# A graph-attention kernel with the logit columns of its weight matrices made by TensorE instead of VectorE, and a new order of its head and tail

## The chip, the cores and the metric

The kernel runs on one core of one Trainium2 chip. The metric is the device time of one execution in microseconds; the kernel before took 2969.14 us (median of three runs, 2966.99 to 2972.52).

## The reference, cut to what matters

```python
# x: 64 x 256 x 512, adj: 64 x 256 x 256 (about 3% ones)
h = relu(layernorm(x))
x = x + gat(gat_elu(h, W1, att_src1, att_dst1, b1), W2, att_src2, att_dst2, b2)   # mask: adj or diagonal
h = relu(layernorm(x))
x = x + relu_att(h, W_proj, W_att, b_att)                                         # mask: adj

def gat(...):                       # per graph; 4 heads of 256 for W1, one head of 512 for W2
    xl = h @ W
    asrc, adst = (xl * a_src).sum(-1), (xl * a_dst).sum(-1)      # one logit per node and head
    e = leaky_relu(asrc[:, None] + adst[None, :], 0.2), masked
    out = softmax(e, axis=source).T @ xl + bias
# relu_att is the same with 8 heads of 64, a vector of 2 x 64 per head in W_att, a bias b_att on the logit
```

A logit is a product of `h` with a column `W[:, head] @ a[head]`. Such columns depend on the weights alone: 4 + 4 of them for `W1`, 1 + 1 for `W2`, 8 + 8 for `W_proj`.

## The kernel before, in words

Each of the 64 graphs has 256 nodes, two tiles of 128 rows. A graph goes through three projections, `m1a` and `m1b` (512 to 1024, two halves), `m2` (1024 to 512) and `m3` (512 to 512). Each is a Strassen-Winograd product of 2 x 2 blocks: seven products `p1` to `p7` on TensorE (PE) of two (`m1`, `m3`) or four (`m2`) fp32 matmuls each, with left operands combined by GpSimd (`left`), right operands (`right`, four subtractions of a weight tile) made once by VectorE, and the partial sums evicted by ScalarE (`q1`, `q6`, `q7`, `q4`) and VectorE (`q2`, `c22`, `q3`). The weights lie in SBUF as `w1_sb` (a, b), `w2_sb` and `wp_sb`, seven blocks each, four of them loaded and three made. The logit columns stand in front of the weights of a block, so that the products yield the logits too.

After a projection a layer goes: exponentials of the logits (`exp`), their rows written to DRAM (`ship`) and read back to all partitions (`rows`), attention weights (`edges`: a scaled copy by ScalarE into one of two PSUM buffers `wys`, then a maximum and mask by VectorE), the matmul with the values (`gat`), and division and bias (`out`). Between layers the features are turned: for most graphs through DRAM (`away`/`home`, `send2`/`take2`) and a VectorE transpose (`back`), for the first and last graph in part by TensorE transposes (`turn`).

The order on every engine's queue is written out by hand. `run` goes through a text of steps such as `0 m1b p2` (graph offset, step, arguments) and issues them; every engine works its own instructions strictly in that order. `head` runs once, `order` for each of 61 rounds, `tail` once. Steps of `w` belong to the class `Weights` (L627 of before). PSUM has four rotating buffers `pm` and two `sum`.

Ahead of `head` stand the loads: graph 0 and the weights on the queues of SP and ACT, the attention vectors each copied to all 128 partitions (L604, L607, L616), and the norm of graph 0. In `head` before, `dots1` (L636) and `dots2` make each logit column by VectorE: `dot` (L595) multiplies a 128 x 256 block of weights with a vector copied to all partitions and sums it, 32 times for `W1` and 32 for `W2`; `columns2` adds halves; `dots3` (L665) multiplies on GpSimd and reduces on VectorE, 16 times. The products of graph 0 that use raw blocks only are issued between them.

## Time and profile before

| what | value |
|---|---|
| median of three runs | 2969.14 us |
| the profiled execution: own time, span | 2968.22 us, 2966.4 us |
| granted TensorE clock, mean of the span | 0.996 |
| PE busy in 0 to 20, 20 to 40, 40 to 60 us | 5.76, 13.54, 12.94 us |
| VectorE busy in 0 to 20, 20 to 40, 40 to 60, 60 to 80 us | 10.30, 17.91, 19.72, 19.48 us |
| ScalarE busy in the same stretches | 3.89, 2.61, 10.43, 6.93 us |
| PE busy in 2900 to 2920, 2920 to 2940, 2940 to 2950, 2950 to 2966.4 us | 20.00, 14.83, 7.96, 6.77 us |
| first PE instruction, last PE instruction start | 11.30 us, 2959.71 us |
| memory traffic in the first 30 us | 200 to 410 GB/s after 3 us |

The span runs from the first to the last instruction of one profiled execution; about 1.8 us of that execution's own time lie outside it. A line of the chain gives start, duration and what ran; PE is TensorE's matmul, DVE VectorE, ACT ScalarE, POOL GpSimd, SP the engine that issues most DMAs. An fp32 matmul shows as two records. "Idle before" names how long an engine stood still ahead of an instruction, and what released it.

### The profile page before, as it was taken

To read this page: it belongs to the slowest core of one execution; us is meant where nothing else is said; L and a number is where in the kernel's file an instruction comes from. 1 tells how busy PE (TensorE), PEld (TensorE's weight loads), DVE (VectorE), ACT (ScalarE), POOL (GpSimd) and SP (SyncE) were. 2 spreads that over 40 slices of the span, in tenths; PEclk is the share of its full clock that TensorE was granted. 3 is DMA by queue.
4 is the path that set the end of the run, shared out by engine and by line. 5 is a ranking of instruction groups with operands and counts; after the bars stand their busy time and mean duration, and the time that the engine had idled before them with its cause. 6 is when DMAs were issued, how large, how long until landed. Compare 5 with 4: busy or idle time off the path is not lost.

```text
span 2966.4 us, 59522 instructions
## 1 busy us (share of the span) xinstructions
PE 2917.8 (98%) x20296; PEld 2531.6 (85%) x20296; DVE 2531.3 (85%) x6370; ACT 1711.3 (58%) x4489; POOL 1287.4 (43%) x1882
## 2 busy tenths in 40 slices
PE   6999999999999999999999999999999999999997
PEld 4888888888888888888888888888888888888886
DVE  8788888888888888888888888888888888888886
ACT  3466565655655655655656556556556556555554
POOL 3443443444444444434444444444444344344433
PEclk9999999999999999999999999999999999999998
DMA  6556555656565665555556565565555556566542
GB/s 193 155 173 180 175 180 171 180 178 179 170 182 176 175 180 174 172 180 177 179 171 185 173 179 173 178 184 167 175 177 174 178 178 179 172 182 176 179 136 73
DMA packets 536859, 513.17 MB, mean 173 GB/s; under 512 B 85736, under 2 KB 373352, under 8 KB 536552
## 3 DMA queue, kind: packets, MB, share of 16 engines
q1 hardware_dynamic: 535176, 507.20, 57.5%
q8 instruction: 165, 2.70, 0.4%
q10 hardware_dynamic: 1376, 2.10, 0.2%
q14 instruction: 142, 1.16, 0.1%
HBM read 332.01 MB, written 168.79 MB: 169 GB/s over the span
## 4 chain that ended last, share of the span: by engine, by line
PE 97%; DVE 1%; DMA 1%; issue 0%; ACT 0%; POOL 0%; SPq 0%; ACTq 0%; DVEq 0%
PE sum L55 38%; PE pm L55 29%; PE pm L411 15%; PE pm L556 8%; PE pm L481 7%; DVE prod L597 0%; DMA w1a_sb<-in_L_gnn_W_dram 0%; DMA xs<-in_x_dram 0%; DMA h<-kept_h 0%; DMA z<-kept_z 0%; DVE e L292 0%; DVE hs L213 0%; ACT h L199 0%; DVE z L419 0%; DMA bc<-kept 0%
## 5 line engine op out<-in xcount | busy, mean ns | idle before, releaser
L291 ACT ACTIVATE wys<-bc,exs_sb 128x256 f32<-128x256 f32 x1646 | 715.4, 468 | 297.4 <-DMA bc<-kept 145.4
L61 ACT ACTIVATE kept<-sum 128x260 f32<-128x260 f32 (+3 forms) x768 | 296.0, 386 | 714.0 <-PE sum L55 713.3
L292 DVE SCALAR_TENSOR_TENSOR e<-wys,exs_sb,cap 128x256 f32<-128x256 f32 x1024 | 444.9, 476 | 62.2 <-ACT wys L291 52.6
L55 PE MATMUL sum<-w_sb,h1s 128*128 128x257 f32 x2048 | 488.1, 380 | 0.6
L411 PE MATMUL pm<-xl,e 128*128 128x257 f32 x2048 | 476.4, 380 | 0.9 <-DVE e L292 0.8
L411 PEld LDWEIGHTS pm<-xl,e 128*128 128x128 f32 x2048 | 387.9, 190 | 60.1 <-DVE e L292 1.7
L55 PEld LDWEIGHTS sum<-w_sb,h1s 128*128 128x128 f32 x2048 | 383.3, 190 | 64.3 <-issue 3.8
L566 POOL TENSOR_TENSOR x<-x,o 128x256 f32<-128x256 f32 x256 | 182.0, 731 | 486.5 <-DVE o L564 484.6
L261 DVE TENSOR_TENSOR xl<-pm,kept 128x256 f32<-128x256 f32 (+2 forms) x768 | 318.1, 415 | 79.1 <-ACT kept L61 40.4
L219 POOL TENSOR_TENSOR hs<-hs 128x256 f32<-128x256 f32 x128 | 109.0, 852 | 617.9 <-DVE hs L213 589.8
L55 PE MATMUL pm<-w_sb,h1s 128*128 128x257 f32 x1536 | 361.6, 384 | 0.0
L55 PEld LDWEIGHTS pm<-w_sb,h1s 128*128 128x128 f32 x1536 | 285.8, 189 | 44.8 <-POOL h1s L219 1.0
L213 DVE STREAM_TRANSPOSE hs<-h 128x512 f32<-128x512 f32 x252 | 283.2, 1150 | 8.4 <-DMA h<-kept_h 8.0
L292 DVE SCALAR_TENSOR_TENSOR e<-wys,exs_sb,mask 128x256 f32<-128x256 f32 x640 | 278.4, 477 | 12.9 <-ACT wys L291 7.0
L449 DVE STREAM_TRANSPOSE h1s<-z 128x512 f32<-128x512 f32 x252 | 260.6, 1104 | 17.6 <-DMA z<-kept_z 17.6
L55 PE MATMUL sum<-w1a_sb,hs 128*128 128x260 f32 x1024 | 269.1, 386 | 4.0 <-DVE w1a_sb L597 3.4
L55 PE MATMUL sum<-wp_sb,hs 128*128 128x264 f32 x1024 | 271.0, 387 | 0.7 <-ACT hs L229 0.7
L55 PE MATMUL sum<-w1b_sb,hs 128*128 128x256 f32 x1024 | 266.4, 383 | 4.9 <-DVE r L417 2.6
L556 PEld LDWEIGHTS pm<-xl,e 128*64 128x64 f32 x8192 | 245.9, 138 | 24.8 <-issue 24.1
L419 DVE SCALAR_TENSOR_TENSOR z<-pm,r,b_sb 128x256 f32<-128x256 f32 x512 | 247.7, 484 | 18.3 <-DVE r L417 0.3
L219 POOL TENSOR_TENSOR h1s<-h1s 128x512 f32<-128x512 f32 x64 | 81.3, 1270 | 412.2 <-DVE h1s L449 405.2
L556 PE MATMUL pm<-xl,e 128*64 128x65 f32 x8192 | 255.8, 223 | 1.9 <-DVE e L292 1.7
(94 smaller groups left out, 4832.0 us busy)
## 6 DMA issues: line engine op xcount, KB each, us to landing
bc<-kept SPq DMA_DIRECT2D x380, 256.0 KB, 4.6
kept_h<-h SPq DMA_DIRECT2D x126, 512.0 KB, 3.5
h<-kept_h SPq DMA_DIRECT2D x126, 512.0 KB, 3.7
kept_z<-z SPq DMA_DIRECT2D x252, 256.0 KB
z<-kept_z SPq DMA_DIRECT2D x252, 256.0 KB, 2.9
xs<-in_x_dram SPq DMA_DIRECT2D x64, 512.0 KB, 6.0
x<-in_x_dram SPq DMA_DIRECT2D x64, 512.0 KB
out_dram<-x SPq DMA_DIRECT2D x64, 512.0 KB
```

The lines of the kernel that those rows point to most:

```text
L55: self.nc.tensor.matmul(to[:, :self.n], self.lhs[:, i, c, :], self.rhs[:, i, c, :], start=(first and c == 0), stop=(last and c == self.nk ...
L61: self.nc.scalar.activation(s[:, :self.n], self.sum[:, :self.n], AF.Copy)
L213: nc.vector.transpose(a[:, 4 * t:4 * t + 2].rearrange("p r k (j q) -> p q (r k) j", q=4), h[:, t].rearrange("p (q i c) -> p q c i", q=4, c=4))
L219: nc.gpsimd.tensor_tensor(s1, s3, a22, ALU.add)
L261: nc.vector.tensor_tensor(dst, pm, add, ALU.add)
L291: nc.scalar.activation(wy, bc, AF.Copy, scale=yw)
L292: nc.vector.scalar_tensor_tensor(dst, wy, xw, mask, ALU.max, op)
L411: nc.tensor.matmul(pm[:, :Q + 1], self.e[1, h][:, s, t * P:(t + 1) * P], xl1[:, s, h, L1:], start=(s == 0), stop=(s == T - 1))
L419: nc.vector.scalar_tensor_tensor(self.zt[t][:, sl], pm[:, :Q], r, b1_sb[:, sl], ALU.mult, ALU.add)
L449: nc.vector.transpose(a.rearrange("p k (j q) -> p q k j", q=4), z.rearrange("p (q i c) -> p q c i", q=4, c=4))
L481: nc.tensor.matmul(pm[:, :n], self.e[2][:, s, t * P:(t + 1) * P], xl2[:, s, half, L2:L2 + n], start=(s == 0), stop=(s == T - 1))
L556: nc.tensor.matmul(pv[q:q + 64, h, :], self.e[3, a * G + h][:, s, t * P + q:t * P + q + 64], xl3[:, s, a * G + h, :], start=(s == 0), stop ...
```

## The change

The attention vectors are no longer copied to all partitions. Six small DMAs on ACT's queue bring them as 32 rows of 128 elements (`vec_sb`). One TensorE transpose turns them, and 26 small ScalarE copies lay them out as stationary operands `va` for the three layers (`lay`), with zeros around a head's entries for layers 1 and 3 (two more memsets on GpSimd).

A block of weights (512 x 128 elements) is turned by four transposes and copied from PSUM by ScalarE (`turnw`, 20 in all: 8 for `W1`, 8 for `W2`, 4 for `W_proj`). `dotw` multiplies it with its part of `va`: one matmul with 8, 2 or 16 stationary and 512 moving columns, accumulating over the blocks of a layer. `cols` copies the sum from PSUM, turns it back with four small transposes and copies the columns into the weight tiles (2 or 4 ScalarE copies). `dot`, `dots1`, `dots2`, `columns2`, `load3` and `dots3` are gone. The subtractions `sums1`, `sums2` and `sums3` remain.

`head` and `tail` are written out anew; `order`, which runs 61 times, is unchanged. In the new head the steps of graph 0's `m1` come after the dots of layers 1 and 2; turning and dots of `W_proj` stand later, among graph 0 and graph 1. In the new tail the same steps stand in another order.

```diff
+    vec_sb = const.tile([32, P], F32, name="vec_sb")
+    va = [const.tile([P, 8, 2, H1], F32, name="va1"), const.tile([P, 4, 2], F32, name="va2"),
+          const.tile([P, 4, 2, 2, G], F32, name="va3")]
+    nc.gpsimd.memset(va[0], 0.0)
+    nc.gpsimd.memset(va[2], 0.0)
...
-    def dot(dst, u, v):
-        prod = work.tile([P, Q], F32, name="prod", bufs=2)
-        nc.vector.tensor_tensor_reduce(prod, u, v, 1.0, 0.0, ALU.mult, ALU.add, dst)
...
+    nc.scalar.dma_start(vec_sb[0:8, :], att_src1.rearrange("h (i f) -> (h i) f", f=P))
+    nc.scalar.dma_start(vec_sb[8:16, :], att_dst1.rearrange("h (i f) -> (h i) f", f=P))
+    nc.scalar.dma_start(vec_sb[16:20, :], att_src2.rearrange("o (i f) -> (o i) f", f=P))
+    nc.scalar.dma_start(vec_sb[20:24, :], att_dst2.rearrange("o (i f) -> (o i) f", f=P))
+    for j in range(2):
+        nc.scalar.dma_start(vec_sb[24 + 4 * j:28 + 4 * j, :].rearrange("i (l k) -> i l k", l=2),
+                            w_att.rearrange("(i l) (j k) -> i j l k", l=2, j=2)[:, j])
 
     graphs[0].load()
-    nc.scalar.dma_start(att1[0].rearrange("p h f -> p (h f)"), rows_of(att_src1, HF))
     for r in range(2):
         bring(w1_sb[1], w1, 2 * Q, r, (nc.sync, nc.scalar))
-    nc.scalar.dma_start(att1[1].rearrange("p h f -> p (h f)"), rows_of(att_dst1, HF))
...
-    for a, src in zip(att2, (att_src2, att_dst2)):
-        nc.sync.dma_start(a, rows_of(src, D2))
...
+        def lay(self):
+            pm = ps_mm.tile([P, 512], F32, name="pm")
+            nc.tensor.transpose(pm[:, :32], vec_sb, ident[:32, :32])
+            for j in range(2):
+                for h in range(H1):
+                    nc.scalar.activation(va[0][:, 2 * h:2 * h + 2, j, h], pm[:, 8 * j + 2 * h:8 * j + 2 * h + 2], AF.Copy)
+                nc.scalar.activation(va[1][:, :, j], pm[:, 16 + 4 * j:20 + 4 * j], AF.Copy)
+                for i in range(4):
+                    for l in range(2):
+                        q = slice(64 * l, 64 * l + 64)
+                        nc.scalar.activation(va[2][q, i, i // 2, 1 - j, 2 * (i % 2) + l:2 * (i % 2) + l + 1],
+                                             pm[q, 24 + 4 * j + i:25 + 4 * j + i], AF.Copy)
...
+        def turnw(self, l, u):
+            pm = ps_mm.tile([P, 512], F32, name="pm")
+            if l == 2:
+                src = [self.block(l, u % 4, u // 4)[:, c] for c in range(4)]
+            else:
+                src = [self.block(l, u, r)[:, k] for r in range(2) for k in range(2)]
+            for c in range(4):
+                nc.tensor.transpose(pm[:, c * P:(c + 1) * P], src[c], ident)
+            self.wt[l, u] = work.tile([P, 512], F32, name="e", bufs=9)
+            nc.scalar.activation(self.wt[l, u], pm, AF.Copy)
+
+        def dotw(self, l, u):
...
+            nc.tensor.matmul(self.acc[l, u // n][:v.shape[1], :], v, self.wt.pop((l, u)), start=(i == first), stop=(i == last))
+
+        def cols(self, l, r=0):
...
+            nc.scalar.activation(flat[:m], self.acc.pop((l, r))[:m, :], AF.Copy)
+            pm = ps_mm.tile([P, 512], F32, name="pm")
+            for c in range(4):
+                nc.tensor.transpose(pm[:, c * m:(c + 1) * m], flat[:m, c * P:(c + 1) * P], ident[:m, :m])
...
     head = """
-        0 turn0, w dots1 0, w dots1 1, 0 m1b p2, w dots1 3, 0 m1b p1, w sums1 1, w dots1 4, w dots1 5, w dots1 6,
-        0 m1a p1, w dots1 2, w dots1 7, 0 m1a p2, w dots2 1, 1 load, w dots2 3, w sums1 0, 0 m1a q1, 0 m1b q1,
...
+        w turnw 1 4, 0 turn0, w turnw 1 5, w lay, w turnw 1 6, w turnw 2 1, w turnw 1 7, w dotw 1 4, w dotw 1 5,
+        w turnw 2 0, w dotw 1 6, 0 edge01, w turnw 2 2, w turnw 1 0, w turnw 1 3, 0 masks, w sums1 1, 0 caps,
+        w dotw 2 0, w turnw 2 3, w turnw 1 1, w dotw 2 1, 0 again, w turnw 2 5, 0 open, w dotw 2 2, w turnw 1 2,
+        w turnw 2 4, w dotw 1 7, w dotw 1 0, w turnw 2 6, w turnw 2 7, w dotw 2 3, w dotw 1 1, w dotw 1 2,
+        w dotw 1 3, w cols 2 0, w dotw 2 4, w dotw 2 5, 1 load, w dotw 2 6, w cols 1, w dotw 2 7, 0 m1b p1,
+        w cols 2 1, 0 m1a p1, 0 m1a q1, w sums1 0, 0 m1b q1, 0 m1a p2, 0 m1a p6, 0 m1a q6, 0 m1a p5, 0 m1a p7,
+        1 stats1 0, w sums2 0, 0 m1a q7, 0 m1b p6, 1 stats1 1, 0 cap3, 0 m1a c22, 0 m1a p4, 0 m1b q6, 1 norm1 1,
+        0 m1a p3, 0 m1a q4, 0 m1a q2, 0 m1b p2, 0 m1b p7, 0 m1a q3, 0 exp1, 0 ship1, 1 norm1 0, w turnw 3 3,
+        0 m1b q7, 0 m1b p5, w turnw 3 0, w sums2 1, w turnw 3 2, 0 rows1, 1 edge01, 0 m1b q2, w turnw 3 1, 1 away1,
+        0 m1b c22, w sums2 2, 0 m1b p3, 1 masks, 0 m1b q3, 0 edges1 1, 0 m1b p4, 0 edges1 2, 0 gat1 1 0, 0 m1b q4,
+        0 out1 1 0, 0 edges1 0, 0 gat1 1 1, 0 out1 1 1, 0 gat1 2 0, 0 edges1 3, 1 home1, 0 gat1 0 1, 0 gat1 0 0,
...
     tail = """
...
-        -1 out2 1, -2 rows3, -1 stats3 1, -2 edges3 0, -1 norm3 0, -2 edges3 1, -1 back3 0, -2 edges3 3, -1 away3,
-        -1 norm3 1, -3 out3 1 1, -1 m3 p1, -1 m3 p2, -2 edges3 2, -2 edges3 5, -1 back3 1, -2 gat3 0 1,
...
-        -1 gat3 0 0, -1 out3 0 0, -1 send2 1 0, -1 edges3 7, -1 gat3 0 1, -1 gat3 1 0, -2 store, -1 out3 0 1,
-        -1 out3 1 0, -1 gat3 1 1, -1 out3 1 1, -1 store, -1 range, -2 range, -1 take2 1 0
...
+        -2 ship3, -2 rows3, -1 out2 0, -1 stats3 0, -1 out2 1, -1 stats3 1, -2 edges3 1, -1 norm3 0, -1 norm3 1,
+        -2 edges3 0, -1 back3 0, -1 send2 1 0, -2 edges3 2, -2 edges3 3, -1 m3 p2, -1 back3 1, -2 range, -1 m3 p1,
...
+        -1 batt3, -2 out3 0 0, -1 exp3, -1 range, -1 edges3 0, -1 edges3 1, -1 edges3 2, -1 edges3 3, -2 store,
+        -1 edges3 5, -1 edges3 6, -1 gat3 0 1, -1 edges3 4, -1 gat3 0 0, -1 out3 0 1, -1 edges3 7, -1 out3 0 0,
+        -1 gat3 1 0, -1 out3 1 0, -1 gat3 1 1, -1 out3 1 1, -1 store
```

## The prediction, made before the changed kernel ran

> **What bounds the kernel now.** I read the page first (busy times, slices, chain), then the waits of PE in the first 160 us, then the chain of work in the head, and last the timelines of head and tail.

> ```profile
> PE 2917.8 (98%) x20296; PEld 2531.6 (85%) x20296; DVE 2531.3 (85%) x6370; ACT 1711.3 (58%) x4489; POOL 1287.4 (43%) x1882
> PE   6999999999999999999999999999999999999997
> PE 97%; DVE 1%; DMA 1%; issue 0%; ACT 0%; POOL 0%; SPq 0%; ACTq 0%; DVEq 0%
> ```

> PE carries the chain. Only the first and the last slice show it idle; in between a graph takes 45.07 us of PE whatever else happens, and neither the loop nor its order changes. So only the head and the tail can move, and I count there what PE loses: idle time, plus the surplus of matmuls at the slow clock, plus PE work that is new. The waits of PE in the first 160 us (engine and line, what it waited for: us, times, longest):

> ```profile
> PE pm L228 <- ACT h L199: 11.3, 1, 11.3
> PE pm L55 <- DVE xl L261: 4.5, 1, 4.5
> PE pm L55 <- issue: 3.8, 2, 2.8
> PE sum L55 <- DVE w1a_sb L597: 3.4, 1, 3.4
> PE sum L55 <- DVE r L417: 2.6, 1, 2.6
> PE sum L55 <- DVE hs L213: 2.2, 1, 2.2
> PE pm L55 <- ACT hs L229: 1.0, 1, 1.0
> PE pm L411 <- DVE e L292: 0.8, 1, 0.8
> PE pm L55 <- DVE w1a_sb L597: 0.7, 1, 0.7
> PE sum L55 <- ACT kept L61: 0.6, 1, 0.6
> ```

> These sum to 30.9 us; 11.3 of it lies before the first instruction, and most of the rest waits for VectorE. The clock shows in the chain (start, us, what, records; an fp32 matmul leaves two records, one per pass):

> ```profile
> 30.81 3.78 PE pm L55 x8
> ...
> 85.30 2.60 PE pm L55 x12
> ```

> A pass of about 256 columns takes 0.47 us in the early head and 0.217 us later. Cold in this sense are the passes from 14.3, 21.5, 24.2, 30.8, 46.3 and 56.2 us: 8+4+8+12+8+8 = 48, which at 0.25 us each is 12, and turn0 some 1 us. The head of before thus loses 30.9 + 13 = 44 us.

> **The change, part by part.** What goes, from VectorE's groups of the first 110 us (line, engine, form, count | busy us, mean ns):

> ```profile
> L597 DVE CUSTOM_DVE_ANT_0 prod<-w_sb,e 128x256 f32<-128x256 f32 x32 | 11.5, 415 | 0.0
> ...
> L671 DVE TENSOR_REDUCE wp_sb<-o 128x4 f32<-128x256 f32 x16 | 5.8, 402 | 0.0
> ```

> 64 dots start 0.345 us apart, 22 us, and with the reductions VectorE is freed of 28 us, POOL of 16 x 0.73 = 12 us, and the loads of some 2 MB of replicated vectors. But the head of before lets PE run 12 of the 14 products of graph 0's first layer under those dots (last one ends at 41.8 us). After, m1 of graph 0 is queued behind nearly all the new PE work, so that cover is gone and the new work stands in the open.

> What comes, on PE: 20 turned blocks of four transposes, 20 dots of 512 moving columns, and the small transposes of lay and cols. The nearest rows (timeline of PE):

> ```profile
> 11.30 1.98 PE L228 MATMUL pm<-ident,h 128*128 128x128 f32 x8 [11.30 <-ACT h L199]
> ...
> 2895.62 1.60 PE L453 MATMUL pm<-ident,z 128*128 128x128 f32 x12
> ```

> A transpose is 0.24 us cold and 0.12 hot (the twelve are followed 1.44 us later), a block 0.96 or 0.48. A dot of 512 columns is two passes of twice 256: 4 x 0.217 = 0.87 hot, 1.89 cold. All of it hot is 9.6 + 17.4 + 1.5 = 28.5 us.

> *Start.* xs landed at 6.8 us with 512 KB of replicated att_src1 beside it on ACT's queue; now 16 KB stand there in six DMAs (about 0.45 us of issue each, ahead of ACT's half of w1b, which nobody needs before 10 us). I take xs 1.5 us earlier (bounds 0 and 2.5). Statistics to norm was 3.6 us, the two norms 1.34, then ACT issues two w1a loads (1.0 to 1.8 as before) and evicts a turned block, the two halves of turn0 and a second block (0.54 each): lay's activations start at 13.7.

> *lay* is 26 tiny ACT instructions. The nearest row is exps: 0.20 for one alone, three in 0.44, so 0.11 apart. I take 2.8 us; if they don't overlap it is 5.2. The first dot needs the 18th of them: 15.5 us. Behind lay on ACT wait the evictions of three blocks, and PE for their PSUM slots; after it ACT (0.54 per block) is faster than PE. The w2 block turned ahead of the first dot needs about 3 MB to have come, by 10 to 11 us at the 350 GB/s of this stretch.

> *Blocks and dots.* The first two dots run cold, to 19.3. Then 11 blocks and 14 dots: 11 x 0.48 + 14 x 0.87 + 0.3 = 17.8 hot, so m1 starts at 37.1 us, 36.1 of it lost. [...] In the trace the clock rose after 3.3 to 5.4 us of plain matmuls, and twelve transposes in a row at 2895.6 stayed hot; a mixture of narrow dots and transposes isn't shown. [...]

> *After.* cols: the flat copy and column copies (ACT) lie under three dots; 0.3 remains. sums1 0 (2.8 us on VectorE) lies under m1a p1 and p2. m1's first nine products end at 37.1 + 9 x 0.87 + 0.3 = 45.2 and the last add 0.5 later; exp1, ship1, rows1 took 7.0 us from exp to the first weighting (41.2 to 48.3) and the first e 1.4 more, so gat1 can start at 54.1. On SP, cap3's transposing loads (3.06 us of issue) and again's load now stand ahead of ship1's store, but what they wait for is done by 40 us. Beneath lie five products and the four blocks of W_proj (4.4 + 1.9), up to 51.5: 2.6 idle, and since 2.6 idle cooled the clock at 56 us and 2.2 didn't at 95, half of a cold start, 0.9. The eight gat1 then run with VectorE's edges, about 7 us as hot work. Later: dots and columns of layer 3, 3.9; stalls like before's 2.2 and 0.8, I take 1.5 (0 to 4). Sum of losses: 36.1 + 0.3 + 1.9 + 2.6 + 0.9 + 3.9 + 1.5 = 47.2, 3.2 more than before.

> *Tail.* Nothing of the work changes, only its order. What the rows show of it (one from the timeline, one from the chain):

> ```profile
> 2931.37 0.80 ACT L199 ACTIVATE h<-x,off,rstd 128x512 f32<-128x512 f32 x1
> ```

> ```profile
> 2950.77 2.08 PE pm L556 x32
> ```

> The second norm of the last graph stood behind two weightings (2.4 us after it could); now it follows the first, but PE is full there. The spread for the last edge stood behind a cold gat3, 1.3 us; now there is room. Four reductions of range, 0.85 us, leave the last chain. The store still waits for the last output. I take 1.5 us gained (0 to 3).

> Sum: +3.2 - 1.5 = +1.7 us. It is made against the profiled execution (span 2966.4, own time 2968.2, 0.9 under the median of 2969.1), and I add it to the median: 2970.8, said as 2971. Own range of this case 2965 to 2976.

> **Rivals.**
> Cold clock (slower). The dots and blocks from 19 us on stay at half rate: 14 x 1.02 + 11 x 0.48 = 19.6 us more, 2990. It decides if the dots still take 0.9 us a pass after about 25 us; if the clock opens halfway, 2980. [...] Against: dots are long and in close order.
> Stalls in front (slower). PE works its queue in order; w2's block, or lay with its 26 instructions, comes 4 to 6 us late, and everything behind it too: about 2977. For it: SP's issues of these loads stood still for 1.2 us at 9.7 and 2.2 us at 12.9; against: 2 MB less to load.
> VectorE's relief pays (faster). rows1 takes 5.4 us (1.92 + 3.44 as in the tail) with SP empty, so its idle time and cold start go (-3.5); no later stalls (-1.5); xs at its early bound (-1); tail at its bound (-1.5); first dots warm sooner (-1). 2971 - 8.5 = 2962.5.
> It does nothing: columns leave VectorE, PE pays what it saves. That is the likeliest case itself.

> **The numbers.** Likeliest 0.54; cold or half cold 0.26; stalls in front 0.11; relief 0.09. A measurement tells 0.2%, 5.9 us, from no change: below 2963.2 is faster, above 2975.1 slower. The likeliest lies inside with all but its edge, the relief is the faster side, the other two the slower: 0.09, 0.54, 0.37. The range takes the half-cold case and most of the cold one: 2963 to 2988.

> **What would show it.** Right: losses of PE in the first 160 us near 47; m1b's first product at 36 to 39 us; dots at 0.43 us a pass after 20 us; lay within 3 us; VectorE's L597 and L671 groups gone with PE's waits for them; a wait of 2 to 3 us for e before the first gat1; the end 1 to 2 us earlier after the last edges. Wrong: m1 after 45 us (clock), a first dot after 19 us (front), no wait at gat1 (relief), or a tail with new idle time, which I have only sketched.

## The result, and the profile after

The changed kernel takes 2977.3 us (median of 14 runs, 2972.2 to 2980.4) against 2969.8 us (14 runs, 2967.0 to 2972.5) for the kernel before on the same chip: ratio 1.0022, 95% interval 1.0015 to 1.0029. It is 7.5 us slower, just past the 0.2% that a measurement can tell. The prediction was 2971 with a range of 2963 to 2988; the time lies in the range, but 1.3 us beyond the likeliest case, which ended at 2976.

The page of the changed kernel: busy time, PE's forty slices, and the chain of work.

```profile
PE 2942.2 (99%) x20433; PEld 2541.0 (85%) x20433; DVE 2500.9 (84%) x6222; ACT 1729.4 (58%) x4551; POOL 1273.6 (43%) x1868
...
PE   8999999999999999999999999999999999999997
...
PE 97%; DMA 2%; DVE 0%; ACT 0%; issue 0%; POOL 0%; ACTq 0%; SPq 0%; DVEq 0%; POOLq 0%
```

The reader is to see that the exchange took place: VectorE is 30 us less busy, PE 24 us more, and PE's first slice went from 6 to 8 tenths. The engine that carries the chain was given the work of one that doesn't.

The waits of PE in the first 160 us of the changed kernel:

```profile
PE pm L662 <- DMA w1b_sb<-in_L_gnn_W_dram: 8.3, 2, 6.4
PE pm L416 <- DVE e L297: 2.7, 2, 1.9
PE pm L662 <- DMA w_sb<-in_L_gnn_W_dram: 2.0, 1, 2.0
PE pm L486 <- DVE e L297: 1.1, 1, 1.1
PE pm L638 <- ACT e L664: 0.6, 1, 0.6
PE pm L662 <- ACT hs L234: 0.2, 1, 0.2
```

These sum to 14.9 us where before had 30.9. The waits for VectorE's dots (L597 before) are gone. In their place stand PE's own new instructions, and two waits for weights. PE's timeline in the head (start, us, what, records, idle before):

```profile
15.96 1.09 PE L662 MATMUL pm<-ident,w_sb 128*128 128x128 f32 x4 [2.01 <-DMA w_sb<-in_L_gnn_W_dram]
...
17.82 2.37 PE L674 MATMUL sum<-e,va 128*8 128x512 f32 x4
20.12 0.66 PE L662 MATMUL pm<-ident,w_sb 128*128 128x128 f32 x4
...
31.45 3.59 PE L674 MATMUL sum<-e,va 128*2 128x512 f32 x8
...
39.27 1.13 PE L55 MATMUL sum<-w1b_sb,hs 128*128 128x256 f32 x4
...
55.91 8.89 PE L416 MATMUL pm<-xl,e 128*128 128x257 f32 x32 [1.91 <-DVE e L297]
64.63 1.04 PE L55 MATMUL sum<-w1a_sb,hs 128*128 128x260 f32 x4
```

Blocks (L662) and dots (L674) fill PE from 15.96 us on. Only behind them comes m1b's first product, at 39.27 us; the first gat1 starts at 55.91, and graph 1's first product at 64.63.

To see where the time went I cut each trace in three: up to the first gat3 group of graph 0 (which opens the steady loop), from there to the 60th gat3 group, and the rest of the span. The last two columns are the loop's excess over 59 times its regular beat of 45.066 us, and how often PE stopped inside the loop's gat3 groups.

| kernel | first gat3 at | loop | rest | span | excess of the loop | stops in gat3 |
|---|---|---|---|---|---|---|
| before | 160.7 | 2663.5 | 142.3 | 2966.4 | 4.6 | 2 |
| changed | 166.9 | 2670.0 | 140.1 | 2977.0 | 11.1 | 7 |
| difference | +6.3 | +6.5 | -2.2 | +10.6 | +6.5 | |

The profiled execution of before took 2968.2 us and that of the changed kernel 2978.7, so the profiles differ by 10.5 us and the medians by 7.5. Each part has its own story: the head lost twice what was predicted, the tail gave what was predicted, and the loop, which the change does not touch, lost as much as the head.

Near its end the tail of the changed kernel reads:

```profile
2967.56 1.66 PE L561 MATMUL pm<-xl,e 128*64 128x65 f32 x40 [0.21 <-DVE e L297]
...
2969.90 0.21 DVE L814 TENSOR_REDUCE top<-ends 128x1 f32<-128x64 f32 x1
```

Between VectorE's last output and its first reduction of top nothing is left; in the kernel before, four reductions of ends stood there (2957.85 to 2958.8 us).

In the loop PE has one kind of wait only. Before and changed, 165 to 2800 us:

```profile
PE pm L556 <- issue: 0.2, 1, 0.2
```

```profile
PE pm L561 <- issue: 3.9, 5, 1.9
```

"Issue" means that PE waited for nothing the profile shows. Around the longest of these stops the changed kernel's timeline reads:

```profile
934.05 3.83 PE L561 MATMUL pm<-xl,e 128*64 128x65 f32 x123
939.73 0.34 PE L561 MATMUL pm<-xl,e 128*64 128x65 f32 x5 [1.85 <-issue]
940.00 5.43 PE L55 MATMUL pm<-w_sb,h1s 128*128 128x257 f32 x16
```

The stop is inside a row of 128 equal matmuls, five before its end. And the sixteen passes behind it take 5.4 us. In the kernel before, the same sixteen took 3.75 us:

```profile
931.85 3.75 PE L55 MATMUL pm<-w_sb,h1s 128*128 128x257 f32 x16
```

That is the clock. Five stretches of the changed kernel (busy us and records of PE, PEld, DVE, ACT, POOL; then the granted clock):

```profile
15.40:18.80 3.40, 2.85 (x10) 1.81 (x11) 1.26 (x2) 3.26 (x19) 1.87 (x3) 0.50 1.07 376
...
52.90:56.40 3.50, 1.59 (x8) 1.01 (x7) 1.30 (x4) 1.49 (x5) 0.00 (x0) 1.00 0.86 251
56.40:59.80 3.40, 3.40 (x9) 2.76 (x9) 2.77 (x8) 2.52 (x7) 0.00 (x0) 0.50 0.37 112
...
937.00:940.40 3.40, 1.55 (x38) 1.32 (x33) 2.19 (x9) 2.54 (x8) 3.00 (x7) 1.00 0.71 249
940.40:943.80 3.40, 3.40 (x10) 2.67 (x9) 3.40 (x7) 0.98 (x4) 2.66 (x4) 0.50 0.43 165
```

Twice PE was busy for only about 1.6 us of a 3.4 us stretch, and twice the next 3.4 us ran at 0.50. Each costs 1.7 us beyond the wait itself: once at the first gat1 (8.7 us until the next product; 7.0 in runs below that stayed hot, that is, at the clock 1.00), once in the loop.

My theory after this: the head pays for PE's new work in series, plus the clock at gat1; the loop pays for instructions that reach PE late in gat3, which the longer program meets in other places. The rivals: the work for the columns costs nothing as such, and the tail or the order is to blame; the clock stayed low in the dots; the loop's extra is chance of one execution.

### The profile page after: what moved, and what is told of

The parts are those of the page before. It is cut to its first block, busy times and chain, and to the rows that moved or that the text cites. A ratio compares the mean times of both kernels' runs of the same rounds, so it can differ in the third digit from the quotient of the medians.

```text
span 2977.0 us, 59697 instructions
## 1 busy us (share of the span) xinstructions
PE 2942.2 (99%) x20433; PEld 2541.0 (85%) x20433; DVE 2500.9 (84%) x6222; ACT 1729.4 (58%) x4551; POOL 1273.6 (43%) x1868
## 3 DMA queue, kind: packets, MB, share of 16 engines
q8 instruction: 166, 2.72, 0.4%
## 4 chain that ended last, share of the span: by engine, by line
PE 97%; DMA 2%; DVE 0%; ACT 0%; issue 0%; POOL 0%; ACTq 0%; SPq 0%; DVEq 0%; POOLq 0%
PE sum L55 37%; PE pm L55 28%; PE pm L416 15%; PE pm L561 8%; PE pm L486 7%; PE sum L674 1%; DMA bc<-kept 0%; DMA h<-kept_h 0%; DMA w_sb<-in_L_gnn_W_dram 0%; PE pm L662 0%; DMA kept_h<-h 0%; DMA kept<-wt 0%; DVE e L297 0%; ACT wys L296 0%; DMA vec_sb<-in_L_gnn_att_dst_dram 0%
## 5 line engine op out<-in xcount | busy, mean ns | idle before, releaser
L61 ACT ACTIVATE kept<-sum 128x260 f32<-128x260 f32 (+3 forms) x768 | 296.4, 386 | 704.0 <-PE sum L55 702.3
L55 PE MATMUL sum<-w_sb,h1s 128*128 128x257 f32 x2048 | 487.8, 380 | 0.6
L55 PEld LDWEIGHTS sum<-w_sb,h1s 128*128 128x128 f32 x2048 | 383.0, 189 | 64.4 <-issue 3.5
L55 PE MATMUL pm<-w_sb,h1s 128*128 128x257 f32 x1536 | 363.8, 385 | 0.0
L55 PEld LDWEIGHTS pm<-w_sb,h1s 128*128 128x128 f32 x1536 | 287.2, 190 | 46.1 <-POOL h1s L224 1.2
L297 DVE SCALAR_TENSOR_TENSOR e<-wys,exs_sb,mask 128x256 f32<-128x256 f32 x640 | 279.0, 479 | 15.0 <-ACT wys L296 14.3
L55 PE MATMUL sum<-wp_sb,hs 128*128 128x264 f32 x1024 | 270.6, 387 | 0.2 <-POOL hs L225 0.2
L55 PE MATMUL sum<-w1a_sb,hs 128*128 128x260 f32 x1024 | 266.4, 383 | 0.0
L55 PE MATMUL sum<-w1b_sb,hs 128*128 128x256 f32 x1024 | 263.1, 379 | 0.0
```

Source lines behind the costliest of these rows:

```text
L55: self.nc.tensor.matmul(to[:, :self.n], self.lhs[:, i, c, :], self.rhs[:, i, c, :], start=(first and c == 0), stop=(last and c == self.nk ...
L61: self.nc.scalar.activation(s[:, :self.n], self.sum[:, :self.n], AF.Copy)
L297: nc.vector.scalar_tensor_tensor(dst, wy, xw, mask, ALU.max, op)
```

## The experiments

Ratios are to the kernel before, on the same chip. Its median was 2966.5 us beside the first four runs and 2970.0 us beside the others, so times of different groups are not compared directly.

**Tail alone, head alone.** The first is the kernel before with the changed `tail` string, the second the changed kernel with the old one.

```
-    tail = """ ... -1 store, -1 range, -2 range, -1 take2 1 0
+    tail = """ ... -1 gat3 1 1, -1 out3 1 1, -1 store
```

> The head and the columns of before, the tail of after. If the tail gives what the two traces show (142.2 us from the last full gat3 of the loop to the end before, 140.0 after), this is 2.2 us faster than before, 2967.5. If that difference was only one execution's, it equals before.

Measured 2966.0 us, ratio 0.9996 (0.9987 to 1.0004). The rest of the span fell from 142.3 to 139.9 us in the trace; the medians show 0.5 us of it, and the interval (-3.9 to +1.2 us) holds both.

> The head and the columns of after, the tail of before. Theory, all of the loss comes with the head: its first gat3 starts 6 us later than in before, as in after (166.9 against 160.7), and without the tail's 2.2 us the kernel takes 2979.5. If the loop's stalls (6.5 us more in the one profile of after) belong to the new tail or to chance, it is 2976 or less.

Measured 2974.8 us, ratio 1.0024 (1.0015 to 1.0033), +8.2 us. The loss comes with the head. But the trace has only +3.3 us in the head itself (first gat3 at 164.0) and +4.4 in the loop, with nine stops in gat3. The loop's share is not chance of one execution, then, or it came twice. The head's steps are those of the changed kernel to the letter, and yet gat1 ran at full clock here, after a wait of 2.15 us:

```profile
55.14 7.20 PE L416 MATMUL pm<-xl,e 128*128 128x257 f32 x32 [2.15 <-DVE e L297]
```

So the half clock at gat1 comes in some executions of this head and not in others.

**No columns of W_proj.** The changed kernel with its four turned blocks, four dots and the column copies of layer 3 left out; W_proj's logit columns are zero, so this part of the computation is missing.

```
-  w turnw 3 3, ... w turnw 3 0, ... w dotw 3 0, ... w cols 3
+  nc.gpsimd.memset(wp_sb[:, :, :, :L3], 0.0)
```

> As after, but the logit columns of W_proj are zeros: its 4 turned blocks, 4 dots and their columns are left out. Theory, new work on PE costs what it takes where PE is full and nothing where PE waits: the dots and columns (0.97 + 2.67 + 0.35 us in the trace of after) go from the time, the four blocks (1.9) don't, since the wait for the first e behind them grows by as much: 4 us less than after, perhaps a cold start on top, 2973 to 2974. My prediction counted all of it as lost: 5.9 less, 2971.4. Rival, the m2 products behind wait for their operands anyway: no change.

Measured 2971.1 us, ratio 1.0014 (1.0008 to 1.0021): 4.5 us more than before, where the changed kernel has 7.5 more (on its own chip) and the head alone, which keeps the old tail, 8.2. So 3.0 to 3.7 us came back, with some 3 us of uncertainty on each comparison: near the 4 us of the theory, but too coarse to tell it from 2 or 5.9, which was the prediction's. The wait ahead of the first gat1 grew to 2.72 us, so the turned blocks were partly filler for it. In the trace the head is only 0.9 us shorter than in the head alone, and 3.9 us shorter than in the changed kernel, of which 1.7 is the half clock at gat1 that did not come here. Most of the difference from the head alone lies in the loop (excess 5.2 us against 9.0), so the run does not show that it is the columns' own time that came back.

**The block as the stationary side.** Each turned block becomes the weights and the vectors (8, 2 or 16 columns) move; the transposes back in cols go. The way the blocks' parts are summed is changed with it, so the logit columns are not those of the reference.

```
-            nc.tensor.matmul(self.acc[l, u // n][:v.shape[1], :], v, self.wt.pop((l, u)), ...)
...
+            for c in range(4):
+                nc.tensor.matmul(self.acc[l, u // n][:, c * m:(c + 1) * m], wt[:, c * P:(c + 1) * P], v, ...)
```

> As after, but the dot takes the turned block as four stationary parts of 128 columns and moves the 8, 2 or 16 vector columns, so that the columns come out in place: no flat copy, no transposes back. If a pass then costs what a transpose of 128 by 128 costs (0.12 us), a block's dot takes 0.96 instead of 0.87 and only the transposes back are saved (1.5 us): about 2976. If the weight load alone sets the pace (half of that), 20 dots save some 8 us, 2968, as far as PE is full there. Rival, the front is bound by ScalarE and loads: no change.

Measured 2989.2 us, ratio 1.0073 (1.0060 to 1.0087). Two windows of its trace, and PE's timeline:

```profile
20.00:40.00 20.00, 20.00 (x99) 20.00 (x98) 0.00 (x0) 8.38 (x19) 0.24 (x1) 0.50 0.41 138
40.00:60.00 20.00, 20.00 (x81) 18.41 (x82) 5.60 (x9) 1.78 (x11) 1.36 (x4) 0.57 0.00 0
```

```profile
38.03 13.65 PE L676 MATMUL sum<-va,e 128*128 128x2 f32 x64
51.55 2.05 PE L55 MATMUL sum<-w1b_sb,hs 128*128 128x256 f32 x4
```

PE and its weight loads show as busy all the time, and the clock stays at half for 41 us. Here the cold clock that the prediction named as a rival is real: m1b starts at 51.6 us. In the changed kernel the same transposes stand between dots of 512 moving columns, and 20 to 40 us ran at 1.00. It is under the narrow passes that the clock did not open: from 38.03 to 51.55 us nothing else ran, and it stayed at 0.50. The transposes are not to blame. In the changed kernel they open it by themselves; its trace has the full clock from 12.01 to 15.42 us, and up to there PE had run nothing but transposes (of blocks and of graph 0's features):

```profile
9.40 1.91 PE L233 MATMUL pm<-ident,h 128*128 128x128 f32 x8
11.11 1.05 PE L662 MATMUL pm<-ident,w1b_sb 128*128 128x128 f32 x4
...
13.29 0.66 PE L662 MATMUL pm<-ident,w1b_sb 128*128 128x128 f32 x4 [0.24 <-ACT hs L234]
```

A block takes 1.05 us at half clock and 0.66 after 12.01 us. In the trace of the stationary blocks the clock averages 0.91 from 0 to 20 us and 0.57 from 40 to 60; by an estimate from these, and from the 0.50 between, it has the same at about 12.9 us. A pass of its dots took 0.21 us at half clock (13.65 us for 64); the pace that the expectation supposes for a weight load alone, half of a transpose's 0.12 us, was not shown.

**Before, shifted by 32 instructions.** The page shows 166 packets of the instruction queue, and the trace 42,183 instructions of PE: 254 per packet. With PE's instructions numbered in the order of the trace, every stop of the loop's gat3 groups so far came at a number that is 193 modulo 256 (193 or 194 in all later runs), 1.3 to 1.5 us after a packet of that queue had ended.

```
+        def fill(self, n, early=1):
+            for _ in range(n):
+                nc.tensor.transpose(idle[:2, :2], ident[:2, :2], ident[:2, :2])
...
+   w fill 16, 0 turn0
```

> The kernel before, with 16 transposes of 2 by 2 ahead of turn0, in the 11 us in which TensorE has nothing to do: 32 instructions more (a weight load and a matmul each), which puts the loop's instructions 288 = 256 + 32 behind before's alignment modulo 256, where the changed kernel has them. Counting TensorE's instructions in the traces, every stop inside the loop's gat3 groups came at an instruction that is 193 modulo 256, some 1.3 us after a packet of the instruction queue ended. If the stops are TensorE's instruction fetch, they fall in this run in the iterations in which the changed kernel had them (6, 17, 19, 21, 28, 30, 39, 41, 50, 52) and no longer at 43 and 54. If the alignment also sets how much is lost, the loop takes 2667 to 2670 us and the median is 2970 to 2973; if how late a fetch comes is chance, or has another cause, the median stays at before's, within 0.1%. If the stops have nothing to do with the fetch, they stay in before's iterations.

Measured 2970.0 us, ratio 0.9998 (0.9989 to 1.0008). One of its two stops, beside the changed kernel's in the same iteration (21):

```profile
1110.94 3.13 PE L557 MATMUL pm<-xl,e 128*64 128x65 f32 x99
1114.53 1.04 PE L557 MATMUL pm<-xl,e 128*64 128x65 f32 x29 [0.46 <-issue]
```

```profile
1118.49 3.13 PE L561 MATMUL pm<-xl,e 128*64 128x65 f32 x99
1122.37 1.04 PE L561 MATMUL pm<-xl,e 128*64 128x65 f32 x29 [0.75 <-issue]
```

After 99 matmuls in both. The stops moved out of iterations 43 and 54 into two of the changed kernel's, 21 and 30, again at 193 modulo 256. I take the stops for PE waiting for its next packet of instructions, since they follow the position in the program and a packet had ended 1.3 to 1.5 us before each; the profile itself names no releaser. But there were two, not seven, and the loop took 2662.3 us: the alignment says where a stop can come, not how much is lost. The half of the expectation that tied the loss to alignment fell. Nor is it a slow transfer in most cases: of the six such packets at the stops that the waits of before and changed list above, four were on the way for 0.93 to 0.97 us, the other two for 1.20 and 1.43, where the median packet of the changed kernel takes 0.96. The packet of the changed kernel's longest stop took 0.93 us; it had started only 0.4 us before PE stood still, so it started late.

**The front reordered.** Loads of the vectors behind w1b's, lay in two parts, the first W2 block behind the first dot.

```
-  w lay, w turnw 1 6, w turnw 2 1, w turnw 1 7, w dotw 1 4, w dotw 1 5
+  w lay, w turnw 1 6, w turnw 1 7, w lay2, w dotw 1 4, w turnw 2 1, w dotw 1 5
```

> The changed kernel with its front reordered: the loads of the attention vectors are issued behind w1b's halves, the 16 small copies of va3 and the two of va2 move behind the fourth turned block of w1b, and the first block of W2 is turned after the first dot. Theory (the front lost 2.2 us to the 2.0 us wait for W2 and to lay's 3.4 us on ScalarE, and everything behind it was queued): first product of m1b at 36.5 to 37.5 us instead of 39.3, median 2 to 3 us under the changed kernel's 2977.3, about 2974.5. Rival (the front is bound by the loads themselves, the DMA engines being busy over 1.0 of their time until 22 us): first product at 38.5 to 39.5 and the median within 1 us of 2977.3.

Measured 2976.2 us, ratio 1.0019 (1.0010 to 1.0028).

```profile
11.23 1.99 PE L233 MATMUL pm<-ident,h 128*128 128x128 f32 x8 [1.85 <-ACT h L204]
...
16.36 1.24 PE L677 MATMUL sum<-e,va 128*8 128x512 f32 x2
...
38.21 1.13 PE L55 MATMUL sum<-w1b_sb,hs 128*128 128x256 f32 x4
...
55.22 7.20 PE L416 MATMUL pm<-xl,e 128*128 128x257 f32 x32 [2.28 <-DVE e L297]
```

The wait for W2 is gone, the first dot is 1.5 us earlier, m1b 1.1 us; norm and turn0 came 2 us later in exchange. The rival, that the front is bound by its loads, was nearer. The eight gat1 took 7.20 us after a wait of 2.28 us, longer than the changed kernel's 1.91. In a later run with this same head (the second of gat3 split) they took 8.89 us after a wait of 2.00.

**Kept warm.** Fillers are matmuls of the identity by itself that nobody reads; seventy of them in the changed kernel, 142 in the head before (with the new tail): the 126 of the expectation and 16 more ahead of graph 1's first product.

```
+                nc.tensor.matmul(to[:, :P], ident, ident, start=True, stop=True)
...
+   w fill 32, w turnw 1 4, w fill 10, 0 turn0 ... w fill 12, w turnw 2 1 ... w fill 16 0, 0 gat1 1 0
```

> The changed kernel with 70 matmuls of the identity by itself, read by nobody, where TensorE waits: 32 before the first turned block, 10 before turn0, 12 before W2's first block, 16 before the first gat1. Theory (clock): in the changed kernel's trace the granted clock was 0.5 from 15.4 to 18.8 us and from 56.4 to 59.8 us, the second after the wait for e, and the first eight gat1 took 8.9 us; kept busy, the clock is 1.0 there, the first dots take 0.43 us a pass instead of 0.6 to 0.9 and gat1 7.2 us: 2 to 3.5 us less, about 2974.5. Rival (the front waits for its loads whatever the clock is, and the half clock at gat1 does not come in most executions): under 1 us. If the 16 before gat1 take longer than the wait, gat1 starts later than 56 us and the gain is lost.

Measured 2977.5 us, ratio 1.0027 (1.0016 to 1.0037).

```profile
54.80 3.73 PE L697 MATMUL pm<-ident 128*128 128x128 f32 x32
58.38 7.10 PE L417 MATMUL pm<-xl,e 128*128 128x257 f32 x32
```

The fillers were mis-sized: each is two passes, and sixteen took 3.7 us. gat1 ran hot in 7.1 us but began 2.5 us later, as the last sentence of the expectation had it. No gain.

> The kernel before with the changed tail and 126 matmuls of the identity by itself in the waits of its head: 44 before turn0, 24 before the first product of m1a, 20 and 8 before two later ones, 30 before m1b's third. Theory (before's head pays for its low clock: products of four passes took 1.9 to 2.1 us until 36 us and 1.04 us after): the products shorten to 1.04 us, the first gat3 comes 2 to 5 us before 160.8, median 2961 to 2964. Rival (VectorE's dots set the pace of before's head, which they filled for 17.9 and 19.7 us of the second and third 20): within 1 us of the 2966.0 of the new tail alone. If a filler runs longer than the wait it fills, up to 2 us more.

Measured 2969.3 us, ratio 0.9995 (0.9986 to 1.0004): no gain over the new tail alone. The same mis-sizing; with most products at 1.03 to 1.14 us in place of 2 the first product of m1a still came after a 1.96 us wait for VectorE. Its first gat3 came at 163.8 us. This fits a low clock that is largely hidden behind VectorE in the head before, but it is no clean test: the fillers themselves ran past the waits, and graph 1's first product came at 60.53 us instead of 56.21. It does not beat the kernel before beyond noise.

**gat3 split.** Two products of layer 2 moved in between the loop's gat3 groups, once with the old head and new tail, once with the reordered front.

```
-  1 masks, -3 gat3 1 1, -1 m2 q7, ... -3 gat3 0 1, 0 edges1 0, -1 m2 p2, ... -1 m2 p4
+  1 masks, -1 m2 q7, -1 m2 p2, -3 gat3 1 1, ... -1 m2 p4, -3 gat3 0 1, 0 edges1 0
```

> The kernel before with the changed tail and, in the loop, two of layer 2's products moved in between the gat3 groups: 64 passes of gat3, eight passes of p2, 32 of gat3, eight of p4, 32 of gat3, where 128 passes of gat3 stood in a row (they take 3.9 us, and 128 weight loads and 128 matmuls are just one 256-instruction packet). Theory (a stop comes when the packet that holds the end of this run is fetched late, about 2.3 us before it is needed): with 3.6 us of long passes in between there are no or nearly no stops inside gat3, the loop takes 2659 to 2662 us instead of 2663.5, and the median is 2 to 4 us under the new tail alone, ratio 0.9983 to 0.9992 to the kernel before. Rival (the stops move to other dense stretches, or the moved products wait for something new): loop 2663 or more, ratio 0.9995 or more.

> The changed kernel with the reordered front and the same split of the gat3 run. Theory (what the new-head kernels lose beyond head and tail, some 4 us in the medians, are fetch stops in gat3: seven to nine of them, 5.7 to 7.0 us, in their traces, against two to four before): the loop takes 2659 to 2662 us instead of 2670 and the median is 4 to 6 us under that of the reordered front alone, ratio 1.0000 to 1.0008 to the kernel before. Rival (the excess has another cause): 0 to 2 us under it, ratio 1.0012 or more.

Measured 3073.3 us, ratio 1.0343 (1.0330 to 1.0357), and 3076.0 us, ratio 1.0352 (1.0338 to 1.0365). Waits and timeline of the first, the waits from 165 to 2800 us:

```profile
PE pm L411 <- DVE e L292: 33.5, 57, 0.6
```

```profile
958.73 2.09 PE L556 MATMUL pm<-xl,e 128*64 128x65 f32 x64
960.74 2.01 PE L55 MATMUL pm<-w_sb,h1s 128*128 128x257 f32 x8
962.68 1.15 PE L556 MATMUL pm<-xl,e 128*64 128x65 f32 x32
963.76 2.01 PE L55 MATMUL sum<-w_sb,h1s 128*128 128x257 f32 x8
```

Half of the theory held: the issue waits inside gat3 are gone altogether (none from 165 to 2800 us in either run), so no stop came without the long dense row. The other half was far off, and so was the rival's number: a graph takes 46.80 us instead of 45.07. Per graph 0.59 us is a new wait for VectorE's e before gat1, presumably since m2's products no longer lie between. And every change between 64-column gat3 and 257-column products costs: the eight passes of p2 hold PE for 1.94 us (960.74 to 962.68) where they take 1.74 in a row, 32 gat3 passes 1.08 where they take 1.0. The remaining part of the 1.73 us I did not trace.

**The changed kernel again.** The kernel itself, a second profile.

> The changed kernel itself, once more, beside the others on the same chip. Both theories: ratio to the kernel before 1.0022 within its interval. Its trace is a second execution of the same program: if the stops in gat3 follow the instruction's position they come in iterations 6, 17, 19, 21, 28, 30, 39, 41, 50, 52 again, at instructions that are 193 modulo 256; if the half clock at the first gat1 groups is a matter of one execution, they take 7.2 us here and the first gat3 comes at 164 to 165 us instead of 166.9.

Measured 2977.4 us, ratio 1.0021 (1.0012 to 1.0029). Its trace: first gat3 at 167.6, loop 2669.2, gat1 8.89 us again after a wait of 2.11 us and a stretch at half clock; seven stops, in iterations 6, 17, 21, 30, 41, 50, 52, every one at 193 modulo 256, and 5.7 us of issue waits. The longest of these:

```profile
2427.84 3.65 PE L561 MATMUL pm<-xl,e 128*64 128x65 f32 x117
2432.69 0.57 PE L561 MATMUL pm<-xl,e 128*64 128x65 f32 x11 [1.19 <-issue]
```

So the loop's extra is not a matter of one execution. The half clock at gat1 came again, and my guess of 7.2 us for the second execution was wrong; but the head alone and the front reordered show that it need not come. The clocks of the unprofiled runs say the same. Each run's mean clock is on record to three places; among the profiled ones with a new head, 0.998 stands only where the trace has no half-clock stretch on record before the tail, and 7 of the 26 runs of the changed kernel have 0.998. Their median is 2976.8 us against 2977.4 for all 26, so the half clock seems to move the median little.

**The wait at gat1 filled.** Seven fillers ahead of the first gat1 of the changed kernel.

```
+   w fill 7 0, 0 gat1 1 0
```

> The changed kernel with seven matmuls of the identity by itself, read by nobody, ahead of the first gat1: in e8 sixteen of them took 3.7 us, so these take some 1.6 us of the 1.9 to 2.1 us in which TensorE waits there for e. In both traces of the changed kernel the granted clock was 0.5 for one stretch of 3.41 us right after this wait and the eight gat1 took 8.9 us. Theory (the wait itself cools the clock): with the wait filled the clock stays at 1.0, the eight gat1 take 7.1 to 7.2 us, the first gat3 comes at 165.2 to 165.9 us instead of 166.9 and 167.6, and the median is about 1.7 us under the changed kernel's 2977.3. Rival (the half clock is set by something else than TensorE's idle time here): gat1 still takes 8.9 us and the time stays.

```profile
54.22 1.72 PE L697 MATMUL pm<-ident 128*128 128x128 f32 x14
56.50 7.20 PE L417 MATMUL pm<-xl,e 128*128 128x257 f32 x32 [0.56 <-DVE e L298]
```

In the trace gat1 takes 7.20 us and the first gat3 comes at 165.0 us, 1.9 and 2.6 us before the changed kernel's, as the theory has it. That does not prove it, since the head alone ran gat1 hot without fillers and reached gat3 at 164.0. The median of six runs is 2978.5 us, ratio 1.0032 (1.0020 to 1.0045), not under the changed kernel's 1.0021. Its loop had an excess of 10.5 us. An interval of 7 us can hardly show a gain of 1.7, least of all over a kernel of which some executions have it already; these runs show none.

The same cut of the traces, for comparison with the medians (difference to the kernel before on the same chip; gat3 split left out). The last column but one says how far the profiled execution lay from the median of its program:

| run | first gat3 | excess of the loop | stops in gat3, us | rest | profiled run against its median | median's difference |
|---|---|---|---|---|---|---|
| before | 160.7 | 4.6 | 2, 0.7 | 142.3 | -1.6 | 0 |
| new tail alone | 160.8 | 4.8 | 4, 2.2 | 139.9 | +0.5 | -0.5 |
| before, shifted | 164.1 | 3.4 | 2, 1.2 | 141.9 | 0.0 | 0.0 |
| old head kept warm | 163.8 | 9.9 | 7, 4.5 | 140.5 | +5.9 | -0.7 |
| changed | 166.9 | 11.1 | 7, 5.6 | 140.1 | +1.4 | +7.5 |
| changed again | 167.6 | 10.3 | 7, 7.2 | 140.8 | +1.8 | +7.3 |
| head alone | 164.0 | 9.0 | 9, 7.0 | 141.1 | 0.0 | +8.2 |
| front reordered | 164.2 | 7.4 | 5, 4.5 | 141.1 | -2.9 | +6.2 |
| kept warm | 166.9 | 7.1 | 6, 4.5 | 141.3 | -1.2 | +7.4 |
| gat1 filled | 165.0 | 10.5 | 6, 4.4 | 140.7 | -0.7 | +8.5 |
| no columns of W_proj | 163.1 | 5.2 | 4, 1.6 | 140.3 | -1.8 | +4.5 |
| block stationary | 180.7 | 6.6 | 8, 4.4 | 141.1 | -0.2 | +22.7 |

A stop's length is counted against the median of the same matmul over the iterations. Between programs with the same head that part can differ by 3 us (before and shifted; changed and head alone), so one trace places a loss, and only the median weighs it. The trace of the old head kept warm is the slowest of that program's eleven executions, so its 9.9 us in the loop are not typical of it.

## Why the prediction was right or wrong

- *PE pays what VectorE saves.* Right, and the reason the change gains nothing: waits of PE fell by 16 us, and about as much new work took their place. The tail alone is no slower, the head alone is; leaving out a fifth of the columns' work (no columns of W_proj) gives back some 3 us, though its trace has most of that in the loop.
- *Dots hot after 19 us.* Right: 8 passes in 3.59 us at 31.45, and the clock was 1.00 from 18.83 to 56.38 us; transposes alone had opened it before, from 12.01 to 15.42 us. The rival came true where the moving side was 2 to 8 columns wide (0.50 for 41 us); the same transposes between dots of 512 moving columns did not bring it.
- *m1 starts at 37.1 us.* It started at 39.27. xs landed 1.9 us earlier (predicted 1.5), but the first dot came at 17.82 instead of 15.5: PE, which takes its queue in order, stood 2.0 us for the first block of W2, which arrived at 15.8 us and not at 10 to 11. (lay's ACT copies took 3.4 us instead of 2.8, the 64x1 ones 0.17 us apiece, not 0.11.) The clock rose at 18.8, so the first two dots took 2.3 us instead of 3.8, and the end of this part is 20.1 instead of 19.3. Then the stretch of blocks and dots took 19.15 us instead of 17.8: a lone dot holds PE for 0.96 us (its two passes stand at 20.71, the next block at 21.67), a block 0.5, and the small transposes of cols 0.33 each, where I had 0.87, 0.48 and 0.3 for all. The sum, 2.2 us, is mis-sized terms, the load of W2 and the narrow work of PE, not a wrong mechanism.
- *gat1 can start at 54.1.* From m1b's first product to the first gat1 it took 16.6 us (predicted 17.0), so it started at 55.9, late only through m1. The wait was 1.9 us (2.6).
- *Half of a cold start at gat1, and about 7 us.* The kernel itself took the whole cold start in both profiled executions (8.7 us), 0.8 more than I had; the head alone took none, so a half was not a bad guess. But I had judged by the length of the wait, and that alone isn't what decides. In the head alone a stretch of 3.45 us in which PE was busy for 1.61 us was followed by a hot one:

```profile
53.30:56.75 3.45, 1.61 (x7) 1.39 (x8) 1.96 (x6) 2.50 (x7) 0.00 (x0) 1.00 0.57 179
56.75:60.20 3.45, 3.45 (x17) 3.02 (x16) 3.34 (x11) 2.62 (x9) 0.24 (x1) 1.00 0.68 248
```

Of the 7.5 us, then: the head and the tail together make 4.1 and 5.4 in the two profiles of the kernel itself, and the loop 6.5 and 5.7. These parts sum to 10.6 and 11.1, more than 7.5, since both profiled executions lie above their median and that of the kernel before below it. The exact division of the median can't be had from them. That the loss comes with the head is shown by the head and the tail alone; that part of it falls in the loop rests on the traces.

## What to carry to other kernels

Work moved from a half-hidden engine to the engine that carries the chain must be counted in series from the moment its consumer is queued behind it; taking 30 us off VectorE bought nothing. A part that a change leaves alone is not thereby constant: before calling a loop fixed, look for the stops in it whose releaser the profile can't name, and compare two executions. When the order of long products and short dense matmuls is changed, measure the beat: four more changes of shape per graph, and the wait they uncovered, cost 1.7 us of 45. A trace is one execution: set its time against its program's median before a part of it is taken as typical.

## What the runs showed of the hardware that was not expected

- In the changed kernel's trace PE's queue of instructions moves 166 packets of 16 KB (2.72 MB) for 42,183 instructions, 254 per packet. At the six stops that the waits of before and changed list, PE goes on 2.3 to 2.9 us after the packet has started: 0.93 to 1.43 us on the way, then 1.3 to 1.5 us more. In a row of 128 matmuls of 64 columns (31 ns each, with as many weight loads) PE passes 256 instructions in 4 us; from 165 to 2800 us of these two traces stops of 0.2 to 1.9 us came there and nowhere else.
- A short stop can cost twice: 1.85 us for the stop at 939.73 us of the changed kernel, and 1.7 us for the half clock after it. The wait of about 2 us before gat1 was followed by the half clock in some executions of a head (8.89 us for gat1 after 1.91, 2.00 and 2.11 us) and not in others (7.20 us after 2.15, 2.28 and 2.72 us). In the two profiles of the changed kernel it lay inside one stretch of the 3.41 us grid; that it lay across a step in hot executions is an estimate for two of them.
- Matmuls with 2 to 8 moving columns and full weight loads, 0.21 us apiece, with transposes among them, left the granted clock at 0.50 for 41 us although PE showed as busy for all of it. For the last 13.5 us before the first product they stood alone.
- Transposes of 128 columns alone opened the clock, in the changed kernel from 12.01 to 15.42 us.
